# Which half messages of a two-layer graph kernel are put off: all of eight batches, or all of five batches and one half of six

## The chip, the cores and the metric

The kernel runs on one core of a Trainium2 chip. The metric is the device time of one execution in microseconds (us), the median over several runs; lower is better. Engines are named as in the profile: PE is TensorE's matrix multiplication and PEld its loading of weights, DVE is VectorE, ACT is ScalarE, POOL is GpSimd, SP is SyncE, which here only issues DMAs.

## The reference, cut to what matters

There are 16 batches `b` of 1024 nodes with 256 features, and one 1024 x 1024 matrix `adj` that serves both layers. It is symmetric in where it is nonzero and sparse. Everything is float32.

```python
# layer 0: dense attention
feats  = einsum('bni,oi->bno', x, W1)
f1     = einsum('bno,o->bn', feats, W2) + b2
coefs  = softmax(leaky_relu(f1[:, :, None] + f1[:, None, :]) + adj, axis=-1)
h      = einsum('bij,bjo->bio', coefs, feats) + bias2 + x
# layer 1: a gate on each edge, and a plain message
S   = sigmoid(relu(h@W1[:d] (of u) + h@W1[d:] (of v) + b1) @ W2 + b2)     # for all u, v
a_t = einsum('buv,bud->bvd', S * adj, h)
m_t = einsum('uv,bud->bvd', adj, h) * h
z   = beta1 * h + beta2 * (a_t @ Wa + ba) + beta3 * (m_t @ Wm + bm)
```

The change concerns `m_t`. Its sum over `u` is a dense product of `adj` with `h`, and its columns `v` (the targets) can be taken in two halves of 512.

## The kernel before, in words

**The plan.** The gates `S` are needed only where `adj` is nonzero, so layer 1's gates are computed edge by edge from lists, and the rest is dense. The work has three stages that overlap.

1. The dense phase, one batch after another (the loop at L1478). For batch `b`: turn `x` (L948), make the features (`pf`, L999), the row of f (`rows_of_f`, tile `pr`, L967), from which ScalarE makes `row` and `col` and VectorE the unscaled coefficients `eT` (L1040); then attention in 8 chunks of 128 rows (`attend`, tile `pv`, L1053), each finished by VectorE into `held[b]` (`keep_h`, tile `xh`). `held[b]` now holds `h`. It is turned (`turn_h`, tile `ph`, kept as `hT`) and multiplied by the sorted layer-1 weights (`end`, tile `pp`) and by `Wa` (`weighed`, tile `pea`). These results go to DRAM on SP's queue as `pu_d`, `pw_d` (stored from `end`) and `ha_d` (from `ea`). In the first 350 us VectorE and POOL also build the edge lists (L838, L845).
2. The scores. Batches form three groups, 0 to 4, 5 to 9 and 10 to 15 (`GROUPS`). For each group, 135 slots are worked through: POOL gathers rows of `pw_d` (tile `gv`, L1212, 5 buffers, fetched 3 slots ahead) and `pu_d` (`gu`), VectorE compares them (L1241), ScalarE sums them (L1255), and POOL scatters the gates into `sa_d` (L1221).
3. The gather stage, for groups 1, 0 and 2 in that order: SP loads slices of `sa_d` (`sat`), ScalarE rearranges them (`apart`, L1338), VectorE multiplies them by `adj` (L1343), and TensorE multiplies with `ha_g` (`pzg` and `pzh`, L1356). SP loads `zb_d`, VectorE adds, ScalarE's queue stores the output.

**The messages.** For a batch and a half of its target columns, `message(b, half, h)` (tile `pm`, L1151) does 8 products for each of two halves `h` of the features, `keep_message` multiplies by `hT` into `mT` on VectorE, and `product` (tile `pz`, L1171) multiplies by `Wm`. `keep_product` adds `beta1 * h` into `zb` on VectorE (L1181), and ScalarE's queue stores `zb_d`. On the chip each float32 matmul appears as two instructions, so one `message` is 16 rows of 512 columns.

**At once or put off.** Messages of batch `b - 1` are either done inside the loop's pass for batch `b`, spread between its attention chunks, or put off. `LATER = (0, 1, 2, 3, 11, 12, 13, 14)` are put off: `put_off` (L1138) stores `held[b]` to `h_d[b]` through SP's queue, and `take_up` (L1142) loads it again later into one of the three buffers `xh`. Then the batch is turned a second time and its messages follow, half after half. In a pass with messages at once, `messages(b - 1, 0, 0)` stands at the boundary between the batches, between `one_end(b - 1, 2, 1)` and `one_end(b - 1, 3, 0)`, while ScalarE and VectorE prepare the next attention.

**What sets the order.** All of it is emitted through one `Timetable`. `times.matmuls` advances a planned clock by 4 / 2400 us a column, `times.at` sets an entry at a planned time, and at the end the entries are sorted by time. This fixes the program order of every engine; the engines then run their queues in order and wait on semaphores. Planned times are not measured times: the plan ends at 2065.9. Group `g` of the scores starts at `paced[g]`, never before `started[g]`, which lies 19 planned us (24 for the last) behind the ends of the group's last batch. Its first gathers are emitted 15 planned us earlier.

After the last batch, three put-off batches (0, 1, 2) fill the planned time until the gather stage begins. The others are laid between the half steps of the gather stage by hand (`follows`, `starts`), and every finished batch frees a buffer for the next `take_up`. One of the three `xh` buffers is used by `load_rest` for a part of group 2's `ha`.

Of the kernel before, what the change touches and what calls it, by code (L numbers as in the profile page):

```python
# [8 lines left out]
F32 = mybir.dt.float32  # L9
# [5 lines left out]
P = 128  # L15
BANK = 512
# [14 lines left out]
HUB = 32  # L31
SEGS = P // HUB
ROUNDS = (11, 10, 6, 5, 4, 4, 4, 4, 4)
LATER = (0, 1, 2, 3, 11, 12, 13, 14)
HALF = 136
R = 2 * HALF

# [334 lines left out]
def edge_layers(  # L372
# [273 lines left out]
    pu_d = [dram.tile([N, n * R], F32, name=f"pu_d{g}") for g, n in enumerate(SIZE)]  # L646
    pw_d = [dram.tile([N, n * R], F32, name=f"pw_d{g}") for g, n in enumerate(SIZE)]
    ha_d = [dram.tile([N, n * D], F32, name=f"ha_d{g}") for g, n in enumerate(SIZE)]
    h_d = {b: dram.tile([P, C * D], F32, name=f"h_d{b}") for b in LATER}
    zb_d = [dram.tile([N, n * D], F32, name=f"zb_d{g}") for g, n in enumerate(SIZE)]  # L650


# [426 lines left out]
    def keep_hT(b, i):  # L1079
        half, at = divmod(2 * i * P, BANK)  # L1080
        if at == 0:
            st["hT", b, half] = dense.tile([P, H, BANK], F32, name=f"hT{half}")
        st["hTi", b, i] = st["hT", b, half][:, :, at : at + 2 * P]
        nc.scalar.copy(st["hTi", b, i], st.pop(("ph", b, i)))  # L1084

# [390 lines left out]
    grows(5)  # L1476
    started = []
    for b in range(B):  # L1478
        at_once = b > 0 and b - 1 not in LATER
        more = b + 1 < B  # L1480

        if b:
            weigh_ends(b - 1, 2)
            one_end(b - 1, 2, 1)
            if at_once:
                messages(b - 1, 0, 0)
            else:
                weigh_ends(b - 1, 3)
            one_end(b - 1, 3, 0)
            one_end(b - 1, 3, 1)  # L1490
            if at_once:
                weigh_ends(b - 1, 3)
            if b - 1 in LATER:
                times.at(times.now, lambda b=b: put_off(b - 1))
            if any(b == lo for lo, _ in GROUPS):
                started.append(times.now + 19.0)
        attention(b, 0)
        if b == 0:
            grows(6, 7)
        if at_once:  # L1500
            messages(b - 1, 0, 1)
        attention(b, 1)
        spreads(b, 0)
        if more:
            times.at(times.now, lambda b=b: load_x(b + 1))
        if at_once:
            products(b - 1, 0, 1)
        if b == 0:
            for i in range(2):
                for h in range(H):  # L1510
                    times.matmuls(2 * R, lambda i=i, h=h: sort_columns(i, h))
            times.matmuls(2 * R, sort_bias)
        attention(b, 2)
        if at_once:
            messages(b - 1, 1, 0)
        turned_ends(b, 0)
        attention(b, 3)
        spreads(b, 1)
        if at_once:
            messages(b - 1, 1, 1)  # L1520
        both_ends(b, 0)
        attention(b, 4)
        if at_once:
            products(b - 1, 2, 3)
        if not more:
            times.at(times.now, lambda: take_up(LATER[0]))
            times.at(times.now + 20.0, lambda: take_up(LATER[1]))
        turned_ends(b, 1)
        if more:
            begin(b + 1, 0)  # L1530
        attention(b, 5)
        both_ends(b, 1)
        if more:
            begin(b + 1, 1)
        attention(b, 6)
        turned_ends(b, 2)
        attention(b, 7)
        for c2 in range(C // 2):
            if more:
# [11 lines left out]
    clears = [(g, k) for g in range(NG) for k in range(pieces[g])]  # L1551
    for n, (g, k) in enumerate(clears):
        times.at(45.0 + 310.0 * n / len(clears), lambda g=g, k=k: clear(g, k))
    made = max(made, started[0] - 30.0)
    times.at(made, list_stack.close)
    gath_stack = ExitStack()
# [43 lines left out]
    messages(B - 1, 0, 1)  # L1600
    messages(B - 1, 1, 0, 3.8)
    products(B - 1, 0, 1)
    b = B - 1
    for n in range(3):
        messages(b, 1, 1)
        turned_ends(LATER[n], 0)
        turned_ends(LATER[n], 1)
        messages(LATER[n], 0, 0, 3.8)
        time = products(b, 2, 3)
        b = LATER[n]  # L1610
        times.at(time + 1.0, lambda b=LATER[n + 2]: take_up(b))
        messages(b, 0, 1)
        turned_ends(b, 2)
        turned_ends(b, 3)
        messages(b, 1, 0, 3.8)
        products(b, 0, 1)
    messages(b, 1, 1)
# [5 lines left out]
    follows = {0: lambda: products(LATER[2], 2, 3)}  # L1623
    starts = {3: 1, 4: 7, 5: 15, 6: 18, 7: 24}

    def opening(b, half):
        turned_ends(b, 2 * half)
        turned_ends(b, 2 * half + 1)
        messages(b, half, 0)

    def whole(b):
        opening(b, 0)
        messages(b, 0, 1)
        turned_ends(b, 2)
        turned_ends(b, 3)
        messages(b, 1, 0, 3.8)
        products(b, 0, 1)
        messages(b, 1, 1)

    follows[15] = lambda: whole(LATER[5])  # L1640
    follows[16] = lambda: products(LATER[5], 2, 3)
    for i, at in starts.items():
        if i == 5:
            continue
        b = LATER[i]
        follows[at] = lambda b=b: opening(b, 0)
        follows[at + 1] = lambda b=b: messages(b, 0, 1)
        follows[at + 2] = lambda b=b: products(b, 0, 1)
        follows[at + 3] = lambda b=b: opening(b, 1)
        follows[at + 4] = lambda b=b: messages(b, 1, 1)  # L1650
        follows[at + 5] = lambda b=b: products(b, 2, 3)
    when = []
    begins = {}
    for i, (g, vc, half) in enumerate(halves):
# [37 lines left out]
            ),  # L1692
        ),
    )
    for i, at in starts.items():
        if i + 2 < len(LATER):
            times.at(when[at] + 2.0, lambda b=LATER[i + 2]: take_up(b))
    times.at(when[starts[6]] + 2.0, load_rest)
# [84 lines left out]
```

## Time and profile before

| | |
|---|---|
| median of 13 runs | 2092.41 us (2088.33 to 2094.52) |
| the profiled execution, its own time | 2093.99 us |
| its span | 2092.3 us |
| mean granted TensorE clock | 0.993 of full speed |
| busy ACT, POOL | 1374.6 us (66%), 1129.5 us (54%) |
| DMA traffic | 644.37 MB, mean 308 GB/s |
| `h_d` stores (`put_off`) | 8 of 1024 KB, 6.0 us to land |
| `h_d` loads (`take_up`) | 8 of 1024 KB, 15.4 us to land |
| `gv` gathers | 405, 7.5 us to land |

How to read it. The page gives each engine's busy time over the span; a TensorE that is "busy" can still run below its best pace, because ends of matmuls are modelled. The busy time in stretches tells the dense phase with messages from that without. The chain and the waits name what a late instruction waited for. A timeline row gives start, length, engine, line, operation, tiles and, in brackets, the idle time before it with its releaser.

### The profile page before, as it was taken

To read this page: it belongs to the slowest core of one execution; us is meant where nothing else is said; L and a number is where in the kernel's file an instruction comes from. 1 tells how busy PE (TensorE), PEld (TensorE's weight loads), DVE (VectorE), ACT (ScalarE), POOL (GpSimd) and SP (SyncE) were. 2 spreads that over 40 slices of the span, in tenths; PEclk is the share of its full clock that TensorE was granted. 3 is DMA by queue.
4 is the path that set the end of the run, shared out by engine and by line. 5 is a ranking of instruction groups with operands and counts; after the bars stand their busy time and mean duration, and the time that the engine had idled before them with its cause. 6 is when DMAs were issued, how large, how long until landed. Compare 5 with 4: busy or idle time off the path is not lost.

```text
span 2092.3 us, 28949 instructions
## 1 busy us (share of the span) xinstructions
PE 2028.8 (97%) x8566; PEld 1553.5 (74%) x8566; DVE 1567.6 (75%) x2348; ACT 1374.6 (66%) x4842; POOL 1129.5 (54%) x986
## 2 busy tenths in 40 slices
PE   7999999999999999999999999899999989999998
PEld 6887888777777768676888886457676666768887
DVE  6798886576777677678878886578788888885544
ACT  4212222386867778587888886568888879886654
POOL 2122221257676777668777776667666756673000
PEclk9999999999999999999999999999999999999999
DMA  6597777778888888789999898899999999997873
GB/s 218 208 339 290 290 294 268 247 249 292 285 281 287 270 288 275 262 302 294 305 312 340 308 316 310 314 385 415 399 384 369 411 416 403 388 403 259 285 235 123
DMA packets 248023, 644.37 MB, mean 308 GB/s; under 512 B 37170, under 2 KB 137522, under 8 KB 245810
## 3 DMA queue, kind: packets, MB, share of 16 engines
q0 software_dynamic: 82528, 349.79, 47.4%
q1 hardware_dynamic: 129506, 258.44, 33.6%
q10 hardware_dynamic: 35824, 34.22, 4.7%
q8 instruction: 69, 1.13, 0.2%
q14 instruction: 96, 0.79, 0.1%
HBM read 479.56 MB, written 162.92 MB: 307 GB/s over the span
## 4 chain that ended last, share of the span: by engine, by line
PE 59%; DVE 13%; DMA 13%; ACT 8%; issue 5%; POOL 2%; ACTq 0%; SPq 0%; POOLq 0%; DVEq 0%
PE pv L1053 18%; PE pm L1151 11%; PE pp L1091 8%; DMA gv<-pw_d,idx_v 7%; PE pzg L1356 5%; DVE gv L1241 5%; ACT gv L1255 4%; PE pf L999 4%; PE pea L1119 4%; PE pz L1171 3%; PE pzh L1356 2%; DMA ha_g<-ha_d 2%; ACT apart L1338 2%; DMA sat<-sa_d 2%; DVE eT L1040 1%
## 5 line engine op out<-in xcount | busy, mean ns | idle before, releaser
L1255 ACT ACTIVATE gv<-gv 128x272 f32<-128x272 f32 x2058 | 856.1, 419 | 304.8 <-DVE gv L1241 201.0
L1241 DVE TENSOR_TENSOR gv<-gv,gu 128x680 f32<-128x680 f32 (+1 forms) x810 | 705.4, 907 | 103.0 <-DMA gv<-pw_d,idx_v 101.5
L1212 POOL DMA_INDIRECT gv<-pw_d,idx_v x405 | 484.2, 1195 | 319.1 <-ACT gv L1255 197.4
L1221 POOL DMA_INDIRECT sa_d<-lg,idx_s x405 | 497.7, 1229 | 132.2 <-issue 104.6
L1053 PE MATMUL pv<-feats,eT 128*128 128x257 f32 x2048 | 470.7, 381 | 6.4 <-DVE eT L1040 5.7
L1151 PE MATMUL pm<-adj_sb,xh 128*128 128x512 f32 x1024 | 454.1, 597 | 2.3 <-DVE xh L1067 2.3
L1053 PEld LDWEIGHTS pv<-feats,eT 128*128 128x128 f32 x2048 | 381.0, 190 | 72.6 <-DVE eT L1040 16.3
L1255 ACT ACTIVATION_READ_ACCUMULATOR gv<-gv 128x1 f32 x2058 | 388.8, 189 | 0.0
L1356 PE MATMUL pzg<-ha_g,apart 128*128 128x256 f32 x1536 | 366.8, 382 | 19.4 <-DVE apart L1343 18.9
L1151 PEld LDWEIGHTS pm<-adj_sb,xh 128*128 128x128 f32 x1024 | 194.6, 192 | 223.0 <-issue 220.1
L1356 PEld LDWEIGHTS pzg<-ha_g,apart 128*128 128x128 f32 x1536 | 288.6, 190 | 79.4 <-DVE apart L1343 31.7
L1338 ACT COPY apart<-sat 128x640 f32<-128x640 f32 (+1 forms) x192 | 264.3, 1390 | 82.5 <-PE pzh L1356 43.4
L1343 DVE TENSOR_TENSOR apart<-apart,adj_sb 128x640 f32<-128x640 f32 (+1 forms) x192 | 166.0, 866 | 128.3 <-ACT apart L1338 127.9
L1091 PE MATMUL pp<-wuv,hT 128*128 128x272 f32 x1024 | 251.0, 395 | 6.2 <-ACT end L1105 4.2
L1091 PEld LDWEIGHTS pp<-wuv,hT 128*128 128x128 f32 x1024 | 194.7, 191 | 53.6 <-issue 6.7
L1040 DVE SCALAR_TENSOR_TENSOR eT<-row,col,grown 128x512 f32<-128x512 f32 x256 | 182.9, 744 | 31.7 <-ACT col L986 30.5
L845 POOL DMA_INDIRECT table_d<-rec,at x52 | 57.4, 1104 | 260.3 <-DVE rec L838 157.6
L1084 ACT COPY hT<-ph 128x512 f32<-128x512 f32 x96 | 55.2, 576 | 113.2 <-PE ph L1073 113.2
L1119 PE MATMUL pea<-wa,hT 128*128 128x256 f32 x512 | 121.0, 379 | 0.0
L1171 PE MATMUL pz<-wm,mT 128*128 128x256 f32 x512 | 116.2, 379 | 1.8 <-DVE mT L1162 1.8
L999 PE MATMUL pf<-w1T,xT 128*128 128x257 f32 x512 | 114.7, 381 | 0.5 <-DVE xT L957 0.5
L1356 PE MATMUL pzh<-ha_g,apart 128*128 128x256 f32 x384 | 114.2, 379 | 0.0
(184 smaller groups left out, 1596.3 us busy)
## 6 DMA issues: line engine op xcount, KB each, us to landing
sa_d<-zero SPq DMA_DIRECT2D x128, 512.0 KB, 5.8
sat<-sa_d SPq DMA_DIRECT2D x128, 320.0 KB, 8.8
sat<-sa_d SPq DMA_DIRECT2D x64, 384.0 KB, 4.8
pu_d<-end SPq DMA_DIRECT2D x64, 272.0 KB, 4.4
pw_d<-end SPq DMA_DIRECT2D x64, 272.0 KB, 5.8
ha_d<-ea SPq DMA_DIRECT2D x64, 256.0 KB, 5.9
zb_d<-zb ACTq DMA_DIRECT2D x64, 256.0 KB, 8.0
xh<-in_x_dram SPq DMA_DIRECT2D x15, 1024.0 KB, 14.2
```

Of the source, the lines that this page charges most:

```text
L999: nc.tensor.matmul(pfs[i], lhsT=st["xT"][:, h, c * P : (c + 1) * P], rhs=w1T[:, h, :], start=(h == 0), stop=(h == H - 1),)
L1040: nc.vector.scalar_tensor_tensor(st["eT", b, k, n][:, i, :], st["row"][:, cols], st["col"][:, j : j + 1], grown[:, j, cols], ALU.max, ALU. ...
L1053: nc.tensor.matmul(pv[:, : D + 1], lhsT=st["eT", b, k, j // 4][:, j % 4, i * P : (i + 1) * P], rhs=st["feats", b][:, j, :], start=(j == 0) ...
L1091: nc.tensor.matmul(pp[:, k, :R], lhsT=st["hTi", b, i][:, h, k * P : (k + 1) * P], rhs=wuv[:, side, h, :], start=(h == 0), stop=(h == H - 1),)
L1119: nc.tensor.matmul(pp[:, k, :], lhsT=st["hTi", b, i][:, h, k * P : (k + 1) * P], rhs=wa[:, h, :], start=(h == 0), stop=(h == H - 1),)
L1151: nc.tensor.matmul(pm, lhsT=held[b][:, c, h * P : (h + 1) * P], rhs=adj_sb[:, c, span], start=(c == 0), stop=(c == C - 1),)
L1212: nc.gpsimd.indirect_dma_start(out=gv, out_offset=None, in_=pw_d[g], in_offset=bass.IndirectOffsetOnAxis(ap=idx_v[:, t, s : s + 1], axis=0),)
L1221: dma = nc.gpsimd.indirect_dma_start(out=sa_d[g], out_offset=bass.IndirectOffsetOnAxis(ap=idx_s[:, t, s : s + 1], axis=0), in_=lg[:, i, : ...
L1241: nc.vector.tensor_tensor(mv, mv, mu, op)
L1255: nc.scalar.activation(one[:, j, :], one[:, j, :], AF.Copy, accum_out=lg[:, i, j : j + 1])
L1338: nc.scalar.copy(apart.rearrange("p g v -> p v g"), sat)
L1356: nc.tensor.matmul(st["pzg", g, vc][j // 4][:, j % 4, :], lhsT=apart[:, j, :], rhs=ha, start=(c == 0 and j % 2 == 0), stop=(c == C - 1 and ...
```

## The change

The same number of half messages, 16, is put off, but others. `WHOLE = (0, 1, 2, 3, 4)` are put off entirely; of `HALVED = (9, 10, 11, 12, 13, 14)` the first half of the target columns is done at once and the second half is put off. The put-off halves form one list, `ITEMS`: (9, 1), both halves of 0 to 4, then the second halves of 10 to 14. Batches 5 to 8 and 15 are done at once entirely, as before. A halved batch needs its `h` again, so 11 batches are stored and loaded in place of 8. The `hT` buffers alternate by turn and no longer by half. The order in which `take_up` and `load_rest` follow each other is a list, `held_next`, and each finished second half frees a buffer.

```diff
-LATER = (0, 1, 2, 3, 11, 12, 13, 14)
+WHOLE = (0, 1, 2, 3, 4)
+HALVED = (9, 10, 11, 12, 13, 14)
+ITEMS = [(9, 1), *((b, half) for b in WHOLE for half in range(2)), *((b, 1) for b in HALVED[1:])]
...
-            st["hT", b, half] = dense.tile([P, H, BANK], F32, name=f"hT{half}")
+            turns = st["turns"] = st.get("turns", -1) + 1
+            st["hT", b, half] = dense.tile([P, H, BANK], F32, name=f"hT{turns % 2}")
...
-        at_once = b > 0 and b - 1 not in LATER
+        at_once = b > 0 and b - 1 not in WHOLE
+        both = at_once and b - 1 not in HALVED
...
-            if b - 1 in LATER:
+            if not both:
                 times.at(times.now, lambda b=b: put_off(b - 1))
...
-        if at_once:
+        if both:
             messages(b - 1, 1, 0)
...
-        if at_once:
+        if both:
             messages(b - 1, 1, 1)
...
-        if at_once:
+        if both:
             products(b - 1, 2, 3)
...
+    started[0] = max(started[0], made + 17.0)
...
+    held_next = [b for b, half in ITEMS[1:] if half or b in WHOLE]
+    held_next = [b for n, b in enumerate(held_next) if b not in held_next[:n]][1:]
+    held_next.insert(held_next.index(HALVED[4]), None)
+
+    def freed(time, b, half):
+        if half and held_next:
+            b = held_next.pop(0)
+            times.at(time, load_rest if b is None else lambda: take_up(b))
+
+    item = (B - 1, 1)
+    for n in range(6):
+        messages(*item, 1)
+        turned(*ITEMS[n])
+        messages(*ITEMS[n], 0, 3.8)
+        freed(finish(*item) + 1.0, *item)
+        item = ITEMS[n]
+    messages(*item, 1)
...
+    frees = {0: ITEMS[5], 15: ITEMS[10], 16: ITEMS[11]}
...
+    for first_of, at in ((6, 1), (8, 7), (12, 18), (14, 24)):
+        for n in range(2):
+            item = frees[at + 3 * n + 2] = ITEMS[first_of + n]
+            follows[at + 3 * n] = lambda item=item: opening(*item)
+            follows[at + 3 * n + 1] = lambda item=item: messages(*item, 1)
+            follows[at + 3 * n + 2] = lambda item=item: finish(*item)
...
+    for at, item in sorted(frees.items()):
+        freed(when[at + 1] + 2.0, *item)
```

`turned(b, half)` is the two `turned_ends` of a half, and `finish(b, half)` its two products.

More of the change, by code (lines that the diff above doesn't have):

```diff
@@ L648, in edge_layers @@
     ha_d = [dram.tile([N, n * D], F32, name=f"ha_d{g}") for g, n in enumerate(SIZE)]
-    h_d = {b: dram.tile([P, C * D], F32, name=f"h_d{b}") for b in LATER}
+    h_d = {b: dram.tile([P, C * D], F32, name=f"h_d{b}") for b in WHOLE + HALVED}
     zb_d = [dram.tile([N, n * D], F32, name=f"zb_d{g}") for g, n in enumerate(SIZE)]
@@ L1522, in edge_layers @@
         attention(b, 4)
-        if at_once:
+        if both:
             products(b - 1, 2, 3)
         if not more:
-            times.at(times.now, lambda: take_up(LATER[0]))
-            times.at(times.now + 20.0, lambda: take_up(LATER[1]))
+            times.at(times.now, lambda: take_up(ITEMS[0][0]))
+            times.at(times.now + 20.0, lambda: take_up(ITEMS[1][0]))
         turned_ends(b, 1)
@@ L1602, in edge_layers, with turned, finish @@
     products(B - 1, 0, 1)
[L1603 to L1617, printed above, removed]
+    def turned(b, half):
+        turned_ends(b, 2 * half)
+        turned_ends(b, 2 * half + 1)
+    def finish(b, half):
+        return products(b, 2 * half, 2 * half + 1)
+    held_next = [b for b, half in ITEMS[1:] if half or b in WHOLE]
[13 more added lines that the diff above has]
+    messages(*item, 1)
     order = [*range(1, NG - 1), 0, NG - 1]
@@ L1622, in edge_layers, with whole @@
     last = halves.index((NG - 1, 0, 0))
-    follows = {0: lambda: products(LATER[2], 2, 3)}
-    starts = {3: 1, 4: 7, 5: 15, 6: 18, 7: 24}
+    follows = {0: lambda: finish(*ITEMS[5])}
+    frees = {0: ITEMS[5], 15: ITEMS[10], 16: ITEMS[11]}
     def opening(b, half):
-        turned_ends(b, 2 * half)
-        turned_ends(b, 2 * half + 1)
+        turned(b, half)
         messages(b, half, 0)
[L1631 to L1651, printed above, removed]
+    def whole(item, behind):
+        opening(*item)
+        messages(*item, 1)
+        turned(*behind)
+        messages(*behind, 0, 3.8)
+        finish(*item)
+        messages(*behind, 1)
+    follows[15] = lambda: whole(ITEMS[10], ITEMS[11])
+    follows[16] = lambda: finish(*ITEMS[11])
+    for first_of, at in ((6, 1), (8, 7), (12, 18), (14, 24)):
[4 more added lines that the diff above has]
+            follows[at + 3 * n + 2] = lambda item=item: finish(*item)
     when = []
@@ L1694, in edge_layers @@
     )
[L1695 to L1698, printed above, removed]
+    for at, item in sorted(frees.items()):
+        freed(when[at + 1] + 2.0, *item)
+    assert not held_next
     for n, (g, c) in enumerate((g, c) for g in order for c in range(C)):
```

## Prediction

> **What bounds the kernel now.** I read first the page's busy times and 40 slices, then the busy time in stretches of 50 us, then the chain in order of time and TensorE's timeline at single batch boundaries.
>
> ```profile
> PE 2028.8 (97%) x8566; PEld 1553.5 (74%) x8566; DVE 1567.6 (75%) x2348; ACT 1374.6 (66%) x4842; POOL 1129.5 (54%) x986
> ```
>
> TensorE is the bound, and the change neither adds nor removes a matmul. So all that can move is the time in which TensorE waits or runs slowly: 2092.3 - 2028.8 = 63.5 us idle, plus slow matmuls inside "busy". The stretches (PE, PEld, DVE, ACT, POOL busy; then clock, DMA share, GB/s) say where:
>
> ```profile
> 700.00:750.00 50.00, 50.00 (x232) 40.55 (x231) 38.75 (x66) 40.06 (x163) 34.63 (x31) 1.00 0.86 291
> 750.00:800.00 50.00, 50.00 (x187) 34.64 (x186) 35.69 (x55) 33.55 (x151) 35.21 (x30) 1.00 0.87 289
> 850.00:900.00 50.00, 47.19 (x166) 31.28 (x165) 32.26 (x51) 28.34 (x128) 33.04 (x31) 0.97 0.76 262
> 1100.00:1150.00 50.00, 48.72 (x236) 41.63 (x235) 42.84 (x76) 39.61 (x166) 35.61 (x32) 1.00 0.97 338
> 1200.00:1250.00 50.00, 47.95 (x221) 40.81 (x220) 43.63 (x76) 40.10 (x164) 36.28 (x32) 0.97 0.91 311
> 1350.00:1400.00 50.00, 45.65 (x132) 24.66 (x133) 39.57 (x46) 35.20 (x157) 32.28 (x27) 0.90 0.95 359
> 1700.00:1750.00 50.00, 43.52 (x167) 30.21 (x166) 41.20 (x48) 41.89 (x137) 28.97 (x22) 1.00 1.03 408
> ```
>
> From 550 to 850 (batches that carry messages) TensorE never rests. It rests at 850 and 1350 (the score groups change), in 1000 to 1250 (batches without messages), and in the gather stage, where the DMA engines are full. The boundary between two batches explains the third. Here is one without messages, then one with them, on TensorE:
>
> ```profile
> 1087.86 1.04 PE L967 MATMUL pr<-ident,f 128*128 128x128 f32 x8
> 1088.73 1.89 PE L1119 MATMUL pea<-wa,hT 128*128 128x256 f32 x8
> 1090.46 2.00 PE L1091 MATMUL pp<-wuv,hT 128*128 128x272 f32 x8
> 1092.29 1.89 PE L1119 MATMUL pea<-wa,hT 128*128 128x256 f32 x8
> 1094.02 2.00 PE L1091 MATMUL pp<-wuv,hT 128*128 128x272 f32 x8
> 1096.84 2.10 PE L1091 MATMUL pp<-wuv,hT 128*128 128x272 f32 x8 [0.82 <-ACT end L1105]
> 1098.78 2.77 PE L1053 MATMUL pv<-feats,eT 128*128 128x257 f32 x12
> 1102.83 8.32 PE L1053 MATMUL pv<-feats,eT 128*128 128x257 f32 x36 [1.28 <-DVE eT L1040]
> ```
>
> ```profile
> 733.43 1.04 PE L967 MATMUL pr<-ident,f 128*128 128x128 f32 x8
> 734.30 1.89 PE L1119 MATMUL pea<-wa,hT 128*128 128x256 f32 x8
> 736.03 2.00 PE L1091 MATMUL pp<-wuv,hT 128*128 128x272 f32 x8
> 737.87 7.03 PE L1151 MATMUL pm<-adj_sb,xh 128*128 128x512 f32 x16
> 744.73 3.83 PE L1091 MATMUL pp<-wuv,hT 128*128 128x272 f32 x16
> ```
>
> From `pr` (the row of f) to the first `pv` of attention lies a chain over ScalarE (`row`, `col`) and VectorE (`eT`). The `pm` of `messages(b - 1, 0, 0)`, 6.87 us from start to start (737.87 to 744.73), covers it; without it TensorE waits for `end` and for `eT`.
>
> To price it I add up, over all matmuls, the start-to-start time above the median of the same shape (0.217 us for 257 columns, 0.429 for 512). From `pr` to `pr` a batch with messages takes 95.10 us, of which 0.12 is lost. The boundaries without messages lose 2.66 and 2.66 (ahead of batches 3 and 4), then with scores running 1.64, 3.08, 2.05 and 4.10 (ahead of 12 to 15). The last holds a half-clock phase (0.97 in the 1200 row). The whole ledger is 87 us: 16.5 in the first 50 us, 7.0 at the first group change (828 to 930), 11.0 at the second (1350 to 1364), 26 in the gather stage from 1450 to 1900.
>
> **The change, part by part.**
>
> *Batches 10 to 15.* `messages(b - 1, 0, 0)` now stands at each of these boundaries. The four stalls, 1.64 + 3.08 + 2.05 + 4.10 = 10.87, go and 4 x 0.12 = 0.5 stays: -10.4. Next late there is VectorE: a halved batch takes 95.10 - 2 x 6.87 - 3.45 (a pair of products) = 77.9 us, with the scores' compares at the same pace. Its VectorE load lies between the rows above (38.75 of 50 with messages, 42.84 without). Between 0 and 1.66 (what batch 6's interval loses at the scores' start) for each of six; I take 0.8 in all, since the message-free batches lose time only at boundaries.
>
> *Batch 4.* Its message leaves the boundary ahead of batch 5. That row will look like those ahead of 3 and 4 (2.66), less the list building's MAX8 and MATCH_REPLACE8 between the `eT` (2.5 us in the 230 us timeline), which end by then. The ends are 0.65 (ahead of batch 2, the lowest) and 4.10; I take 2.0, so +1.9.
>
> *Work moved.* In all, 16 halves are put off before and after, each with 2 turnings, 2 `pm` groups and 2 products; the built order on TensorE behind the dense phase is the same row for row. In timetable terms group 0 starts at 381.0 instead of 387.9, group 1 at 878.0 (882.6) and group 2 at 1350.2 (1351.3); a slot of group 1 gets 3.50 instead of 3.47 us. The `hT` buffers alternate by turn, as they did by half. No price.
>
> *First group change (7.0 us).* VectorE waited there on arriving `gv` (23.6 us of the 820 to 940 window, longest 8.7): the last slot's gather is issued after five prefetches of the next group. That order stays. The stores of batch 9 come 34 us of timetable earlier after the change, but POOL waited for them 0.3 us at most, so nothing is to be had from that. What differs is TensorE's work beside it: the end of batch 10 instead of its first half. From 0 to 11.0 (the other change): -7 to +4; I take 0, by its own row.
>
> *Three more put-offs.* 1 MB stores on SP's queue in batches 5, 10 and 11; landing takes 6.0 us. In batch 5 the store stands ahead of the last `pw_d` store, which group 0's first gather needs. That gather was issued at 370.2 and lands 7.5 us later by the page's median, while the first compare ran at about 386: 8 us of slack for a store of 6.0, so 0; without the slack 6.0. The others pass `ha_d` alone, needed hundreds of us later.
>
> *Three more take-ups.* 1 MB loads, 15.4 us to land. The first extra one (batch 2) waits on SP for `zb` of batch 9, which VectorE gives only behind the second group change, at about 1355 us; five `ha_g` loads are queued behind it. They are not needed before the gather stage at about 1437, but they come in one burst while group 2's first `gv` fly. Price 0 to 7.6 (`ha_g` took 19.0 there, the late `gv` 11.4); I take 1.0, because the burst of one `xh` and four `ha_g` at 1370 cost TensorE nothing in the ledger. The two others fall into the gather stage (five and `load_rest` instead of three and `load_rest`), with batch 12 and `load_rest` some 12 us apart. At 408 GB/s, 1.05 MB occupy all engines for 2.6 us, 5.1 for both; nothing if hidden. TensorE is idle 6.5 of 50 us in the worst row and about 6% over the stage, so most of it hides; I take 1.8. Each load is issued 40 us or more ahead of its turning, so none is waited for itself.
>
> A rule that speaks against this part: the Trainium skill, DMA: Bandwidth & Descriptors, "Rules for kernel authors", says that spreading DMAs over issuing engines does not help bandwidth because all share the same 16 engines. By it alone SP's extra 3 MB would push POOL's gathers back in full; at the page's 435 GB/s that is about 7.2 us, an estimate, and the sum would come to -0.5. The share of 1.03 in the 1700 row agrees that they are full there.
>
> The clock: at 880 us TensorE ran 8.80 us on a `pm` group that takes 7.03 elsewhere, after an idle of 2.27 us. The Trainium skill, TensorE: Matmul & The Clock Gate, "HAM oscillation", puts the danger at idle gaps above about 3.4 us; this case's row shows it already at 2.27. By the rule the 0.8 to 1.3 us waits would never cost clock, by the row a slightly longer one does.
>
> Sum: -10.4 + 0.8 + 1.9 + 1.0 + 1.8 = -4.9. The profiled execution took 2093.99 us (span 2092.3); the median is 2092.41, 1.6 lower. As a difference within one ledger it applies to either: 2089.1 against the profiled one, 2087.5 against the median.
>
> **Rivals.** (1) *The gain is given back where it is made:* halved batches still stall, because compares and `eT` share VectorE (42.84 of 50 busy without messages). With the 1.66 in each of six batches: -10.4 + 10.0 + 1.9 + 2.8 = +4.3 at worst, at half of it -0.7: 2091.7. Against it: batch 11's interval, with scores and messages, loses 0.12. (2) *The first group change goes too,* because TensorE does not need VectorE at that moment: a further -7.0, 2080.5. For it: only one 2.3 us wait of TensorE (`pm` on `xh`) began it. Against: VectorE is late all the same. (3) *Slower: DMA.* The burst at 1355 delays group 2's first `gv` as `ha_g` was delayed, +7.6, and both loads of the gather stage are paid in full, +5.1: -10.4 + 0.8 + 1.9 + 12.7 = +5.0, 2097.4. It decides against the change once loads cost more than 7.7 us. Against it: the quiet burst at 1370. (4) That the change does not do what it says: the built order shows the `pm` groups moved as described, and no matmul more or less; excluded.
>
> **How the numbers follow.** The forecast (2083 to 2090) has 0.49, rival 1 has 0.27, rival 2 has 0.12, rival 3 has 0.12. This kernel's runs can tell about 0.2% (4.2 us) from no change, so faster means under 2088.2. Of the forecast 0.40 lies there, with rival 2's 0.12 and 0.02 of rival 1: 0.54. Slower (over 2096.6) takes 0.08 of rival 3 and 0.03 of rival 1: 0.11. The rest is 0.35. The range 2079.5 to 2095 holds the forecast, rival 2, rival 1 up to about +2.6, and leaves out most of rival 3.
>
> **What would show it.** In the profile after: batch boundaries from about 990 to 1250 us like the 733 row, TensorE at 50.00 in most of those stretches; a new wait for `eT` near 362 us; 11 `h_d` stores and 11 loads; idle at the two group changes about as before; the gather stage's idle up by 2 us or so. I am wrong if TensorE still waits for `eT` or `end` in batches 10 to 15, or if the stretch 1300 to 1400 loses much over 11 us.

## The result, and the profile after

The changed kernel took 2105.7 us (median of 11 runs, 2101.5 to 2107.3) against 2092.55 for the kernel before, now over 50 runs: a ratio of 1.0059, 95% interval 1.0051 to 1.0067. (The ratios are those on record, with their intervals; they need not equal the quotient of the two medians beside them, here 1.0063.) The prediction, 2087.5 with a range up to 2095, was wrong, and in sign. The profiled execution took 2107.28 us (span 2105.6).

The page's busy times of the kernel after:

```profile
PE 2029.9 (96%) x8566; PEld 1555.1 (74%) x8566; DVE 1566.8 (74%) x2348; ACT 1373.7 (65%) x4842; POOL 1134.1 (54%) x986
```

The work is the same; TensorE's idle time grew from 63.5 to 75.7 us. The same stretches as before (PE, PEld, DVE, ACT, POOL busy; clock, DMA share, GB/s):

```profile
700.00:750.00 50.00, 50.00 (x173) 32.26 (x172) 39.27 (x60) 34.73 (x149) 34.68 (x31) 1.00 0.87 294
750.00:800.00 50.00, 50.00 (x234) 41.12 (x233) 36.35 (x61) 40.76 (x163) 32.21 (x29) 1.00 0.83 265
850.00:900.00 50.00, 42.01 (x175) 32.12 (x174) 32.50 (x57) 32.74 (x135) 30.63 (x29) 0.93 0.74 251
1100.00:1150.00 50.00, 49.25 (x206) 36.62 (x204) 36.02 (x61) 39.65 (x165) 36.32 (x31) 1.00 0.90 295
1200.00:1250.00 50.00, 47.90 (x182) 34.94 (x181) 39.79 (x61) 35.71 (x153) 37.87 (x30) 0.97 0.87 284
1350.00:1400.00 50.00, 43.41 (x129) 23.65 (x130) 39.16 (x45) 32.75 (x147) 30.96 (x26) 0.93 0.88 340
1400.00:1450.00 50.00, 46.29 (x155) 29.40 (x154) 31.73 (x37) 33.92 (x132) 26.94 (x26) 0.97 1.01 397
1700.00:1750.00 50.00, 41.56 (x168) 31.39 (x167) 34.57 (x41) 36.63 (x121) 22.65 (x20) 0.97 1.03 399
```

Stretches of equal time hold somewhat different work in the two kernels, but four rows stand out: 850 (42.01 against 47.19), 1350 (43.41 against 45.65), 1400 (full before) and 1700 (41.56 against 43.52). The batches from 1100 to 1250 hardly rest less than before. The 1400 row of the kernel before:

```profile
1400.00:1450.00 50.00, 50.00 (x185) 34.22 (x184) 39.06 (x47) 40.78 (x157) 31.20 (x26) 1.00 1.02 413
```

The prediction's ledger (time from start to start above the median of the matmul's shape) puts it in its place:

| part of TensorE's order | lost before | lost after | difference | predicted |
|---|---|---|---|---|
| start and batches 0 to 3 | 24.7 | 22.7 | -2.0 | 0 |
| batches 4 and 5 | 2.8 | 2.8 | 0 | +1.9 |
| batch 6 | 1.7 | 0.1 | -1.6 | 0 |
| batches 7 to 9 | 0.3 | 0.3 | 0 | 0 |
| batch 10, with the first group change | 7.0 | 12.4 | +5.4 | 0 |
| batches 11 to 15 | 10.9 | 9.3 | -1.6 | -9.6 |
| second group change and put-off work up to the gather stage | 11.4 | 16.8 | +5.4 | +1.0 |
| gather stage, all three groups | 28.6 | 35.7 | +7.1 | +1.8 |

Two rows are gains that the prediction did not have. The 2.0 us at the start lie within what this stretch varies by over all 16 profiles (some 2.5 us by the same sum). Batch 6's 1.6 us went with batch 4: in the run below that puts off batch 4 and halves nothing, its interval loses 0.1 as well.

The boundaries themselves did what was forecast. TensorE, ahead of batch 14 in the kernel after, to be laid beside the rows at 1087 and 733 of before:

```profile
1118.13 1.04 PE L969 MATMUL pr<-ident,f 128*128 128x128 f32 x8
1119.01 1.89 PE L1122 MATMUL pea<-wa,hT 128*128 128x256 f32 x8
1120.73 2.00 PE L1094 MATMUL pp<-wuv,hT 128*128 128x272 f32 x8
1122.57 7.03 PE L1154 MATMUL pm<-adj_sb,xh 128*128 128x512 f32 x16
1129.43 3.83 PE L1094 MATMUL pp<-wuv,hT 128*128 128x272 f32 x16
1133.10 1.89 PE L1122 MATMUL pea<-wa,hT 128*128 128x256 f32 x8
1134.83 3.64 PE L1055 MATMUL pv<-feats,eT 128*128 128x257 f32 x16
```

No bracket: `pm` covers the chain to `eT`, and nothing waits. But one attention chunk later in such a batch, at 1231 us:

```profile
1225.01 3.64 PE L1055 MATMUL pv<-feats,eT 128*128 128x257 f32 x16
1228.49 0.59 PE L1174 MATMUL pz<-wm,mT 128*128 128x256 f32 x2
1231.18 4.97 PE L1174 MATMUL pz<-wm,mT 128*128 128x256 f32 x14 [2.10 <-DVE mT L1165]
```

`pz` waits for `mT`, which stands on VectorE behind compares that wait for `gv`; TensorE then runs some of them at half pace (14 `pz` take 4.97 us, 3.29 behind the same kind of wait at 1150, where it does not).

The first group change on TensorE and on VectorE:

```profile
872.05 5.09 PE L1001 MATMUL pf<-w1T,xT 128*128 128x257 f32 x12 [6.15 <-DVE xh L1069]
877.47 2.10 PE L1094 MATMUL pp<-wuv,hT 128*128 128x272 f32 x8 [0.33 <-ACT feats L1030]
```

```profile
869.06 1.65 DVE L1244 TENSOR_TENSOR gv<-gv,gu 128x680 f32<-128x680 f32 x2 [12.22 <-DMA gv<-pw_d,idx_v]
870.62 0.68 DVE L963 TENSOR_TENSOR xh<-xh,bias_bc 128x512 f32<-128x512 f32 x1
871.22 0.16 DVE L1066 RECIPROCAL inv<-pv 128x1 f32<-128x1 f32 x1
871.42 0.48 DVE L1069 SCALAR_TENSOR_TENSOR xh<-pv,inv,xh 128x256 f32<-128x256 f32 x1
```

The same place in the kernel before, on VectorE and on TensorE:

```profile
877.61 1.65 DVE L1241 TENSOR_TENSOR gv<-gv,gu 128x680 f32<-128x680 f32 x2 [8.66 <-DMA gv<-pw_d,idx_v]
```

```profile
880.00 8.80 PE L1151 MATMUL pm<-adj_sb,xh 128*128 128x512 f32 x16 [2.27 <-DVE xh L1067]
```

A compare of the old group's last slot blocks VectorE for 12.22 us (8.66 before). Behind it in VectorE's order are the additions of the bias to `x` and the finishing of the last chunk, for which TensorE waits. POOL tells why that gather came so late:

```profile
849.59 0.96 POOL L1208 DMA_INDIRECT gu<-pu_d,key_u  x1 [0.30 <-DMA ha_d<-ea]
850.85 0.94 POOL L1215 DMA_INDIRECT gv<-pw_d,idx_v  x1 [0.30 <-issue]
852.10 0.94 POOL L1215 DMA_INDIRECT gv<-pw_d,idx_v  x1 [0.30 <-ACT gv L1258]
853.34 1.02 POOL L1215 DMA_INDIRECT gv<-pw_d,idx_v  x1 [0.30 <-issue]
857.02 0.93 POOL L1215 DMA_INDIRECT gv<-pw_d,idx_v  x1 [2.65 <-ACT gv L1258]
858.25 1.01 POOL L1224 DMA_INDIRECT sa_d<-lg,idx_s  x1 [0.30 <-issue]
859.57 0.96 POOL L1208 DMA_INDIRECT gu<-pu_d,key_u  x1 [0.30 <-issue]
860.83 0.94 POOL L1215 DMA_INDIRECT gv<-pw_d,idx_v  x1 [0.30 <-issue]
```

The first five are the new group's prefetches; the last `gu` and `gv` of the old group stand behind them, at 859.57 and 860.83. The Trainium skill, Perfetto Trace Analysis, "Tensor Engine Instruction (MATMUL, LD_WEIGHTS)", calls ACT, DVE and GPSIMD strict FIFO; the rows agree.

The third loss lies in ScalarE's queue, behind the second group change:

```profile
1411.94 0.43 ACT L1258 ACTIVATE gv<-gv 128x272 f32<-128x272 f32 x1 [2.18 <-DVE gv L1244]
...
1421.66 0.37 ACTq L1190 DMA_DIRECT2D zb_d<-zb  x1
1422.07 0.43 ACT L1258 ACTIVATE gv<-gv 128x272 f32<-128x272 f32 x1 [9.61 <-DMA sat<-sa_d]
```

A sum does not read `sat`. What waited is the `zb_d` store ahead of it. A semaphore is a counter by which an engine learns that something is done. In the trace the transfers of SP's and ScalarE's queues take eight completion semaphores in turn, and a transfer is issued only when the one that used its semaphore last has landed. Here that was a `sat` load, issued at 1406.17 us and landed at 1421.64; the store followed at 1421.66. Ahead of that load SP had issued two `take_up` and six `ha_g` from 1358 to 1393 us. ScalarE stood still for 9.61 us, and TensorE waited 3.24 us for it:

```profile
1421.28 1.89 PE L1174 MATMUL pz<-wm,mT 128*128 128x256 f32 x8
1426.41 3.54 PE L1174 MATMUL pz<-wm,mT 128*128 128x256 f32 x8 [3.24 <-ACT hT L1087]
```

The fourth has the same form: an output store at 1739.53 us with `[7.47 <-DMA xh<-ha_d]` behind it on ScalarE, that is, a store whose semaphore belonged to `load_rest` (issued at 1720.43, landed at 1739.46). TensorE then waits 3.49 us for `apart` at 1746.28.

### The profile page after: what moved, and what is told of

Same layout as the page of the kernel before. It is cut to its first block, busy times and chain, and to the rows that moved or that the text cites. A ratio compares the mean times of both kernels' runs of the same rounds, so it can differ in the third digit from the quotient of the medians.

```text
span 2105.6 us, 28951 instructions
## 1 busy us (share of the span) xinstructions
PE 2029.9 (96%) x8566; PEld 1555.1 (74%) x8566; DVE 1566.8 (74%) x2348; ACT 1373.7 (65%) x4842; POOL 1134.1 (54%) x986
## 3 DMA queue, kind: packets, MB, share of 16 engines
HBM read 482.71 MB, written 166.07 MB: 308 GB/s over the span
## 5 line engine op out<-in xcount | busy, mean ns | idle before, releaser
L1224 POOL DMA_INDIRECT sa_d<-lg,idx_s x405 | 507.6, 1253 | 137.9 <-issue 104.5
L1174 PEld LDWEIGHTS pz<-wm,mT 128*128 128x128 f32 x512 | 99.0, 194 | 27.7 <-DVE mT L1165 7.6
```

The source lines that it names most:

```text
L1174: nc.tensor.matmul(pz[:, k, :], lhsT=st["mT"][:, h, at : at + P], rhs=wm[:, h, :], start=(h == 0), stop=(h == H - 1),)
L1224: dma = nc.gpsimd.indirect_dma_start(out=sa_d[g], out_offset=bass.IndirectOffsetOnAxis(ap=idx_s[:, t, s : s + 1], axis=0), in_=lg[:, i, : ...
```

## The experiments

Theory: each loss comes from the order in which POOL, SP and ScalarE issue transfers, and can be taken away alone. The rivals differ by run: VectorE's load, the bytes on the DMA engines, or a stall that comes back elsewhere. The kernel before ran beside them on the same chip, with medians from 2090.9 to 2094.3; ratios are to it, with their intervals.

Losses are those of one profiled execution of each kernel, which can lie some 6 us from its median (2096.19 against 2102.05 in the first run below, 2104.97 against 2098.98 in the second). What the expectations call group 1's gather stage runs from the first `pzg` to about 1765 us in the profile after. By the kernel's order group 1 ends there at 1699 us, so this stretch holds the first steps of group 0 too, and the wait at 1746 is one of group 0's. It is called the first part of the gather stage here.

**zb stores on SP's queue, behind the dense phase.**

```diff
-        nc.scalar.dma_start(
+        (nc.sync if "tail" in st else nc.scalar).dma_start(
...
+    times.at(lead - 0.3, lambda: st.update(tail=True))
```

> The changed kernel, with the zb stores behind the dense phase issued from SP in place of ScalarE. In the program every transfer that SP or ScalarE issues waits until the one issued eight places earlier, on either, has landed. Theory 1 (a ScalarE store is stuck behind a slow load): the 9.6 us wait of ScalarE at 1412 to 1422 us and the 7.5 us one ahead of 1746 us were zb stores waiting for a sat load and for load_rest. Without them the stalls of TensorE at 1426 (3.2 us) and 1746 (3.5 us) go, with the half-clock phases behind them: 2096 to 2099 us, 7 to 10 less than the changed kernel's 2105.7. Rival (the additional megabytes themselves: full DMA engines delay gv and sat, whoever issues the stores): both stalls stay, within 2 us of 2105.7.

Measured: 2102.05 us, 1.0043 [1.0029, 1.0057]. The stretch up to the gather stage lost 11.3 us instead of 16.8, as before the change, and the stall at 1426 is gone: it belongs to the store. The gather stage hardly moved (its first part: 28.6 instead of 28.9). The time fell between the two expectations; its interval overlaps that of the changed kernel (1.0051 to 1.0067), so the stall's end is plainer in the profile than in the time.

**First gathers 14 instead of 15 planned us ahead of a group.**

```diff
-            times.at(time - (15.0 if k == 0 else 0.0), first)
+            times.at(time - (14.0 if k == 0 else 0.0), first)
```

> The changed kernel, with the first gathers of a score group emitted 14.0 planned us ahead of its start and not 15.0, so that on GpSimd the last gu and gv of the old group stand ahead of the five first gathers of the new one. Theory (the group change costs what it costs because the last slot's gv is issued behind five prefetches): VectorE's wait there (12.2 us at 857 to 869, in the kernel before 8.7) falls to under 5 us, and the time lost by TensorE at the first change (12.4 us) and the second (10) by 5 to 8 each: 2090 to 2096 us. Rival (the new group's own gathers are late, so the order is indifferent): the wait moves to the new group's first slots and the time stays within 2 us of 2105.7.

Measured: 2098.98, 1.0028 [1.0018, 1.0038], 3 us above the theory's range. The first change lost 3.3 us instead of 12.4. The second did not gain (19.7 up to the gather stage, 16.8 without the edit): there the old group's last fetch is planned 13.9 to 14.0 us ahead, so 14.0 still puts the prefetches first. Hence 13.0 below.

**One part of the change alone: batch 4 put off in place of batch 11, in the kernel before.**

```diff
-LATER = (0, 1, 2, 3, 11, 12, 13, 14)
+LATER = (0, 1, 2, 3, 4, 12, 13, 14)
```

> The kernel before, with batch 4 put off in place of batch 11: the changed kernel's early part alone, with no half batch and no more transfers than before. Theory 1: nothing is dearer in the gather stage, so it loses what the kernel before loses there; the first group change falls on other work (VectorE's wait is the same kind), so it may move by 5 us either way, and the boundary ahead of batch 12 gains 1.6: 2086 to 2097. Rival (moving the first group change against the batches is what costs): the time lost between the row of f of batch 10 and of batch 11 rises by 5 or more, and the total goes to 2097 or more with the gather stage unchanged.

Measured: 2094.88, 1.0012 [0.9999, 1.0026]. With no batch halved the first change lost 10.7 us (7.0 before): group 0's scores start about 8 us earlier, so the change falls on another piece of TensorE's order. VectorE and TensorE in this run:

```profile
868.73 1.64 DVE L1241 TENSOR_TENSOR gv<-gv,gu 128x680 f32<-128x680 f32 x2 [11.99 <-DMA gv<-pw_d,idx_v]
```

```profile
872.52 5.97 PE L1091 MATMUL pp<-wuv,hT 128*128 128x272 f32 x16 [8.26 <-ACT hT L1084]
```

So the first change became dearer with batch 4's shift alone, in this one profile; the time is not clear of no change. VectorE's wait is also longer than before, 11.99 for 8.66 us.

**More halves: batches 7 to 14 halved, 0 to 3 put off entirely.**

```diff
-WHOLE = (0, 1, 2, 3, 4)
-HALVED = (9, 10, 11, 12, 13, 14)
+WHOLE = (0, 1, 2, 3)
+HALVED = (7, 8, 9, 10, 11, 12, 13, 14)
...
```

(`ITEMS` and the place of `load_rest` follow from these.)

> The changed kernel with batch 4 done at once again and the second halves of batches 7 to 14 put off: the halving alone, 12 stores and loads, the first group change again close to where the kernel before has it relative to the batches (two batches ahead of it are now halved). Theory 1 (stuck stores and a dearer gather stage): the loss behind the dense phase stays at 50 us or more, against 40 in the kernel before: 2098 to 2108. Rival (the first group change is the cost): the dense part keeps the gain of the boundaries, 8 to 10 us, and the total is at 2092 or below.

Measured: 2108.85, 1.0086 [1.0071, 1.0102], just above the theory's range. So halving costs without batch 4's shift. The loss sits in the gather stage, 40.2 us for 35.7; the first change lost 8.3. Each further half is one more store and load, but that these make the price is not shown by this run.

**The store of a halved batch 35 planned us later.**

```diff
-                times.at(times.now, lambda b=b: put_off(b - 1))
+                wait = 35.0 if at_once else 0.0
+                times.at(times.now + wait, lambda b=b: put_off(b - 1))
```

> The changed kernel, with each halved batch's store to h_d issued 35 planned us behind the batch boundary instead of at it. Theory (SP's burst at the boundary delays POOL's gathers): VectorE's waits for gv between 900 and 1250 us fall from 39 us to about 20 (before: 18.7), the waits of 5 to 7 us about 10 us behind three boundaries go, TensorE's losses in batches 11 to 15 fall by 4 to 5 us of 9.4, and the time comes to 2100 to 2102. Rival (VectorE's own load, compares and coefficients together, makes the waits): they stay at 35 to 40 us and the time at 2104 to 2107.

Measured: 2106.61, 1.0063 [1.0049, 1.0078]; VectorE's waits for `gv` between 900 and 1250 stayed at 40.6 us (18.7 before, 39.4 after). The theory of the burst at the boundary falls, and the rival's numbers hold. Its cause does not: VectorE is less busy there (36.02 of 50 us in the 1100 row, 42.84 before). That it therefore reaches a compare earlier and waits longer fits, but no run shows it. TensorE does not lose all of these waits, 39.4 us; it loses where something that it needs is queued behind the waiting compare.

**First gathers 13 ahead, in both kernels** (the edit above with 13.0).

> The changed kernel, with each group's first gathers emitted 13.0 planned us ahead of its start instead of 15.0, so that at both group changes POOL issues the old group's last gu and gv ahead of the new group's five prefetches. Theory (that order makes the group changes dear): the first change loses about 3 us instead of 12.4, the second 3 to 8 instead of 16.8, and the time comes to 2090 to 2098. Rival (the change of groups is dear because group g+1's first gathers arrive late whatever their order): what is won at the old group's last slot is lost at the new group's first, both changes stay within 3 us of theirs, time 2099 to 2106.

> The kernel before, with the same edit: first gathers 13.0 planned us ahead instead of 15.0. Theory: its first group change loses about 2 us instead of 7.0 and its second 5 to 10 instead of 11.4, so the time is 2082 to 2089. Rival (first gathers late whatever their order): 2091 to 2095.

Measured: after, 2093.24, 1.0000 [0.9990, 1.0010]; before, 2084.13, 0.9960 [0.9945, 0.9976]. POOL at the first change of the kernel after with this edit:

```profile
848.23 0.96 POOL L1208 DMA_INDIRECT gu<-pu_d,key_u  x1 [0.30 <-DVE inv L1066]
849.50 0.94 POOL L1215 DMA_INDIRECT gv<-pw_d,idx_v  x1 [0.30 <-issue]
850.74 1.57 POOL L1224 DMA_INDIRECT sa_d<-lg,idx_s  x1 [0.30 <-issue]
854.67 0.96 POOL L1208 DMA_INDIRECT gu<-pu_d,key_u  x1 [2.35 <-DVE gv L1244]
```

The old group's last pair now leaves at 848.23 and 849.50, some 11 us earlier, ahead of the new group's `gu` at 854.67. The first change lost 3.0 us instead of 12.4; at the second the wait of 6.90 us at 1356 is gone, one of 3.30 us at 1366 is new, and 7.4 instead of 16.8 are lost up to the gather stage. In the kernel before, the first change gained nothing that is clear (6.2 for 7.0, and 7.7 in a second profile of the same kernel, from the last pair of runs below), while the second went from 11.4 to 0.4 (2.8 in the second profile). There the expectation met the time but not its parts, which were 2 us for the first change and 5 to 10 for the second: that the sum came out is luck. So the order of prefetches cost the kernel before at the second change, and the changed one at both. With the edit in both, the changed kernel is still 0.4% slower by these two ratios, which were taken side by side.

**load_rest one freed buffer later.**

```diff
-    held_next.insert(held_next.index(HALVED[4]), None)
+    held_next.insert(held_next.index(HALVED[5]), None)
```

> The changed kernel, with load_rest and the take-up of batch 13 exchanged in held_next, so that load_rest comes one freed buffer later. Theory (the output store waits on a load that is eight issues older, and load_rest at 1720 is that load): the stall of 3.5 us at 1746 and the 6.6 us lost in that half step go or move to a later half step at a lower price, group 1's stage loses 23 to 25 us instead of 28.9, time 2101 to 2104. Rival (the stage is short of DMA bandwidth, the order of loads is indifferent): group 1's stage loses 27 to 31, time 2104 to 2108.

Measured: 2099.48, 1.0029 [1.0017, 1.0042], somewhat better than the theory's range. The wait at 1746 is gone (0.40 us left at 1746.89), and the first part of the gather stage lost 24.1 us instead of 28.9 (the whole stage 31.5 instead of 35.7).

**Bare bytes: three more 1 MB transfers in the kernel before.** They go from `h_d` of batch 0 to an unused place in DRAM.

```diff
+    copied = dram.tile([P, C * D], F32, name="copied")
+    def copy(b):
+        nc.sync.dma_start(out=copied, in_=h_d[b])
...
+    for at in (1350.0, 1580.0, 1760.0):
+        times.at(at, lambda: copy(0))
```

> The kernel before with three more transfers of 1 MB on SP's queue, from h_d of batch 0 to an unused place in DRAM, at 1350, 1580 and 1760 planned us, where the changed kernel has about its three more loads. It prices bare bytes. By the prediction's own terms (1.0 + 1.8) 2095 to 2096; if the DMA engines are full and each transfer is paid, 7 to 11 us more, 2100 to 2104; if it is the order of issue that costs and not the bytes, under 1.5 us more, 2092 to 2094.

Measured: 2096.72, 1.0026 [1.0015, 1.0036]: 4.6 us over the kernel before beside it, between the prediction's terms and full payment. Bytes cost something; they do not make 13 us. By the profile this run reads and writes as much of the chip's memory as the changed kernel, 482.71 and 166.07 MB. But the transfers go from DRAM to DRAM, and their stores fall behind 1350 us and not in the dense phase, so this is the price of a neighbour, and not the price itself. The Trainium skill, DMA: Bandwidth & Descriptors, "Rules for kernel authors", says that transfers of all issuing engines run on the same 16 DMA engines. The prediction's estimate from that and the page's bandwidth, with nothing hidden, was 7.2 us; the measured 4.6 lies below.

**The three edits together, and zb stores and 13.0 together in the kernel before.**

> The changed kernel with the three edits that were tried singly together: first gathers 13.0 planned us ahead, zb stores behind the dense phase on SP's queue, load_rest one freed buffer later. Theory (each stall has its own cause in the order of issue, so the gains add): first change 3 us, second change with the put-off work behind it 1 to 4 instead of 16.8, group 1's gather stage 23 to 26 instead of 28.9, time 2082 to 2086. Rival (the DMA engines are full behind 1320 us, and a stall that is taken away comes back elsewhere): no better than first gathers 13.0 ahead alone, 2091 to 2094.

> The kernel before with first gathers 13.0 planned us ahead and zb stores behind the dense phase on SP's queue. In the kernel before with the first edit alone no store of ScalarE's queue held TensorE up at the second change (0.4 us lost there), so the second edit should bring 0 to 2 us by the theory that the stuck store belongs to the changed kernel's bursts: 2082 to 2085. If the stores were in the way in every kernel: 2079 to 2081. It is also the bar that the changed kernel with its three edits has to pass.

Measured: 2086.87, 0.9977 [0.9967, 0.9987], and 2088.67, 0.9979 [0.9967, 0.9991]. The single gains in the medians (12.5 + 3.6 + 6.2 = 22.3) nearly add: 18.8. The gather stage lost more than in any of the three single runs, 33.5 us in its first part, on TensorE at 1438:

```profile
1431.58 0.59 PE L1359 MATMUL pzh<-ha_g,apart 128*128 128x256 f32 x2
1438.27 3.78 PE L1359 MATMUL pzg<-ha_g,apart 128*128 128x256 f32 x8 [6.09 <-DVE apart L1346]
```

ScalarE's `apart` there waits 6.04 us for a `sat` load that SP issued at 1413.09 us and that landed at 1435.97. Ahead of it SP had issued a zb store at 1408.54, a `take_up` at 1411.05 and another zb store at 1411.42; that the zb stores held it up is a guess, which the last experiment bears on. The first run lies 0.9 us above the theory's range. In the kernel before, the zb stores on SP were expected to win a little or nothing, 2082 to 2085; 2088.67 is above that, and no faster than with 13.0 alone (2084.13, and 2086.62 below).

**Products 0 and 1 of a halved batch behind chunk 2,** added to the three edits.

```diff
         attention(b, 2)
+        if at_once and not both:
+            products(b - 1, 0, 1)
```

(and `if both:` instead of `if at_once:` at their place behind chunk 1)

> The same with one more edit: in a halved batch's pass products 0 and 1 stand behind attention chunk 2 instead of chunk 1, which gives mT 3.5 us more. Theory (what is left of the dense phase's losses is pz waiting for an mT that stands on VectorE behind compares waiting for gv): the waits of pz for mT near 1140 and 1221 us go, batches 11 to 15 lose 3 to 5 us instead of 6 to 9, the time is 2 to 4 us below the run without this edit. Rival (the wait moves to the next tile that VectorE owes, eT or xh): within 1 us of it.

Measured: 2082.31, 0.9956 [0.9941, 0.9971], 4.6 us below the run without it, though the two intervals overlap. Batches 11 to 15 lost 4.8 us instead of 8.9. TensorE in such a batch:

```profile
1141.77 3.62 PE L1174 MATMUL pz<-wm,mT 128*128 128x256 f32 x16
1145.23 0.60 PE L1075 MATMUL ph<-ident,xh 128*128 128x128 f32 x4
1147.76 3.72 PE L1055 MATMUL pv<-feats,eT 128*128 128x257 f32 x16 [1.93 <-DVE xh L1069]
```

`pz` no longer waits for `mT`; part of the wait moved on to `xh`, as the rival said, but at a lower price.

**zb stores back on ScalarE, the other three edits kept; and the kernel before with 13.0 once more.**

> The changed kernel with first gathers 13.0 ahead, load_rest one freed buffer later and products 0 and 1 behind chunk 2, but zb stores on ScalarE's queue again. In the run with the three edits a zb store on SP's queue stood among the loads of sat near 1436 us, TensorE waited 6 us there, and group 1's gather stage lost 33.5 us. Theory (a zb store costs on either queue, on SP by holding up sat loads, on ScalarE by holding up sums): group 1's stage loses 24 to 27 instead of 31.1, the stretch ahead of it 6 to 8 instead of 1.6, time 2080 to 2085, within 3 us of the run with zb stores on SP. Rival (the stores on SP were free): 2085 to 2089.

> The kernel before with first gathers 13.0 planned us ahead, the same kernel as in the run of that edit alone, for a comparison on one chip: 2083 to 2087 by its first run. If the changed kernel's two halves are of use once their stalls are gone, the other kernel of this call is below it; if the extra loads cost as much as the boundaries bring, the two are within 2 us.

Measured: 2085.19, 0.9976 [0.9967, 0.9985], and 2086.62, 0.9974 [0.9962, 0.9985]. The first time lies just outside the theory's range and just inside the rival's, so it does not decide. The profiles, one of each kernel, speak for the theory that zb stores cost on either queue: on ScalarE 8.8 us are lost up to the gather stage and 25.5 in its first part, on SP 1.6 and 31.1. These two kernels, run side by side, are equal. The best changed kernel (0.9956) and the kernel before with one constant changed (0.9960 and 0.9974) cannot be told apart: once repaired, the change brings nothing that these runs can show.

## Why the prediction was wrong

Four terms of the sum failed, each too low: the stalls left in batches 10 to 15 (by 8.0 us in the two profiles), the first group change (5.4), the take-ups at the second change (4.4) and the gather stage (5.3). In the first, waits inside a halved batch were priced at next to nothing. In the other three, moved work and loads were taken to leave what stands behind what in the queues nearly as cheap as before. Batch 4's term was too high by 1.9, and the start and batch 6 gained 3.6, so the sum missed by 17.6.

**Batches 10 to 15 (-10.4 and +0.8).** The four boundary stalls went, and `pm` covers `eT` as argued. The residual was mis-sized: priced at 0.8 us and the 0.5 left at the boundaries, it measured 9.3 in the profile after and 6.5 and 6.0 in two runs that differ from it only behind 1320 us (zb stores, load_rest). The net gain over the kernel before's 10.9 is 1.6 to 4.9 us instead of 9.6. The prediction said that the message-free batches lose time only at boundaries and carried that over; in halved batches 5.7 of the 9.3 us sit at two stops of `pz`, which needs `mT` from a VectorE that waits for `gv`. This is rival 1 by size, but not by cause: it blamed VectorE's load, and VectorE is waiting, not busy.

**Batch 4 (+1.9).** 0: its interval lost 0.1 before and after. The lower end taken, 0.65, was still too high. (It is the loss ahead of batch 1, not 2; ahead of 2 the same sum gives 3.8.)

**First group change (0, range -7 to +4).** +5.4 in the two profiles; 10.6 to 12.4 us in three profiles of kernels that are changed alike up to there, against 7.0 and 8.2 in two of the kernel before (its own and the run with copies), so +2.4 to +5.4. The prediction saw the order on POOL, and group 0's earlier start, 381.0 for 387.9, but took the old price because the order stayed. It did not ask what lies at the new moment. The run with batch 4 alone shows that the shift is enough, and the run with 13.0 that the order is needed for it. How much of the rise comes from VectorE's longer wait (12.22 for 8.66) and how much from the TensorE work that stands behind it, no run separates.

**Take-ups at 1355 (+1.0, range 0 to 7.6).** The burst came as described, and the second change itself cost the same (11.0 both times). The price appeared 65 us later, by a path the prediction did not have: a zb store on ScalarE behind a load. 5.4 us, gone when the store moves.

**Gather stage (+1.8, range 0 to 5.1).** +7.1 in the two profiles. 4.8 us left its first part when only the order of two loads changed, and with them the worst wait, an output store behind `load_rest`. That loads are early enough for their own turning is true and was not the question; what stands behind them on their semaphore was. The sum for this stage is the least certain: over profiles of kernels without the extra loads it lost 28.6 (before) to 36.5 us, and 34.5 with batch 4 put off and nothing halved. So part of the 7.1 may be that the kernel before's profile is a low one.

**Put-offs (0).** Not contradicted: delaying the stores of the halved batches changed nothing that the time shows (2106.61 for 2105.7).

**Rivals.** Rival 3 had the sign, and its 2097.4 was the nearest figure, but its mechanism, late first `gv` and bytes paid in full, is not what was found: bare bytes cost 4.6 us, and three changes of order alone took 18.8 us away. Rival 2 fell. The list of what would show it wrong named the wait that came, in batches 10 to 15, with the wrong tile, but it expected the group changes as before and 2 us in the gather stage, where the three largest losses came.

What stays open: how much of the gather stage's loss is bytes, order or the spread of single executions, why there the single gains did not add in full, and why VectorE's waits for `gv` doubled beside halved batches.

## What to carry to other kernels

When work is moved in a plan with several in-order queues, the bytes and the covered waits can be the smaller part of the sum, as they were here: ask for each queue what now stands behind the moved transfers, including waits that the program adds for completion semaphores, and who needs the engine that issues them. An event like a change of groups keeps its order and still changes its price when its moment shifts, so look at what the bound engine does at the new moment. And before crediting a change, mend what both versions share: here one constant made the kernel before 0.3 to 0.4% faster, and the change, once repaired, added nothing to that.

## What the runs showed of the hardware

The clock after an idle gap. This takes, over all 16 profiles and behind 60 us, each TensorE matmul that came more than 1.6 us later than the median pace, and the six start-to-start times from it on. Up to 2.0 us late, these ran at their usual pace, except in three cases where TensorE was slow already (at about 1355, behind a longer wait). From 2.0 to 3.5 us about half of the cases (20 of 37) took 1.36 to 2.10 times the usual time, the others at most 1.19 times. So 2.10 us of idle time at 1231 did it, while a matmul 3.00 us late at 1022 in the run with the later store was followed by the usual pace. Above 3.5 us all 24 cases were slow, 1.57 times or more. The Trainium skill, TensorE: Matmul & The Clock Gate, "HAM oscillation", gives the rule of no idle gaps above some 3.4 us. Above that the cases here agree; below it they do not, since about half of those from 2.0 to 3.5 us were followed by slow matmuls. What decides between 2.0 and 3.5 us no run here shows.

A store can stop an engine's computing through a load on another engine's queue: in this program, where the two queues take eight semaphores in turn, ScalarE stood still for 9.61 and 7.47 us behind stores whose semaphore belonged to a load of SP that landed 15.5 and 19.0 us after its issue.
